# Second normalized rows through DRAM in 32 by 32 blocks, and zeros only behind the ends of the lists

## The chip, the cores and the metric

The kernel runs on one core of a Trainium2 chip. A core has five engines with an instruction stream each: TensorE (PE in the profile) multiplies matrices into PSUM, VectorE (DVE) and ScalarE (ACT) work element by element, GpSimd (POOL) does the same more slowly and issues indirect DMAs, and SyncE (SP) only issues DMAs. Sixteen DMA engines serve all queues. The metric is the device time of one execution in microseconds; lower is better.

## The reference

Four batches of 512 tokens with 512 features, in float32:

```python
x = x + tanh(g_xattn) * attention(layernorm(x), ctx)      # 16 heads of 32, 64 keys, causal mask
xf = layernorm(x)                                         # the "second" normalization
scores = softmax(xf @ gate_w.T); weights, idx = top_k(scores, 2)      # 8 experts
y = sum over the two chosen experts e of weight * (silu(xf @ w1[e].T) * (xf @ w3[e].T)) @ w2[e].T
z = (silu(xf @ ws1.T) * (xf @ ws3.T)) @ ws2.T             # the shared expert, for every token
x = x + tanh(g_ffn) * (y + z)
```

A layernorm subtracts the row's mean and divides by the root of its variance plus 1e-5; it has no learned scale. A product contracts over the features, so TensorE needs the rows turned: features on the partitions, tokens along the free dimension.

## The kernel before

**Attention and routing.** `attention()` makes four passes, b = 0 to 3. Pass b scores the queries of batch b in two halves of two token tiles (`score_products`, `largest`, `exponentials`, `softmax`), turns the probabilities (`transpose_p`) and forms their products with the values (`attend`). Between these it projects the queries of batch b+1 (`project_q`), which keeps TensorE supplied. From pass 1 on it also finishes batch b−1, called `last`: `project_out` adds the attention onto x; `moments` and `deviation` give mean and rstd; `second_rows_of` normalizes its four tiles on VectorE; `turn` transposes them on TensorE, 16 products with the identity, and ScalarE copies them to `x2t[last]`; `gate` multiplies the turned rows with the router's weights, `gate_sum` adds four partial products, and `choose` picks two experts a token in some 26 small VectorE instructions, with `attend` of the pass written between them. In the next pass `route` turns the choice into places (one product counts the tokens ahead within a tile, another the tiles ahead), and GpSimd scatters every row, with its weight and address behind it, to two places of the DRAM table `xg_d`: each expert has a region of 2048 rows there. `softmax` uses GpSimd for its last multiply, so it shares that queue with the scatters. `last_routing()` does the same for batch 3, where `fill(n)` puts n products of the shared expert in between.

**The order inside a row.** `normalize(..., turned=True)` stores a row's 32-blocks with two indices swapped. A later fetch of 128 listed rows in four DMAs (`fetch`), followed by one VectorE instruction that transposes 32 by 32 blocks (`turn` at line 882), then gives the experts turned rows. In this kernel TensorE turns the swapped rows as they are, and so `second_rows` loads the router's weights and the shared expert's first weights (`sh13`) with the same swap, in 4 and 8 DMAs.

**Zero rows.** An expert's list ends inside a tile of 128 rows, and the rest of the tile must hold zeros. Nine DMAs at line 253 write zeros into all of `xg_d`, 17,280 rows of 2112 bytes, and one at line 257 into `y_d`, which collects the experts' results. Every scatter waits for the zero fill.

**Experts.** `tile_table` counts the tiles of each expert on VectorE. Then come 34 tiles of 128 rows (32 at least): `fetch`, `turn`, two up products in 8 instructions of TensorE (`hidden`), the gated product, `turn_g`, `down`, and two indirect adding DMAs by GpSimd. At the end the shared expert's down products and y are added and stored.

**What sets the order.** In attention, routing and experts the streams of TensorE, VectorE, ScalarE and GpSimd follow the program as it is written (`manual_schedule`). SP's order up to the experts is set by a scheduler at build time; each queue executes in order, and an instruction that waits holds up all behind it. `sh13` lies in the memory of `wq_sb` and so waits for the last query product. The experts' weights wait for memory of the attention to come free.

Of the kernel before, what the change touches and what calls it, by code (L numbers as in the profile page):

```python
# [13 lines left out]
F32 = mybir.dt.float32  # L14
I32 = mybir.dt.int32
# [4 lines left out]
P = 128  # L20
# [10 lines left out]
TOPK = 2  # L31
CAP = B * S

MAXT = (TOPK * B * S + NE * (P - 1)) // P
MINT = TOPK * B * S // P
ROWS = NE * CAP + (MAXT - TOPK * B * S // P) * P

# [10 lines left out]
def gated_cross_attention_moe(  # L48
# [48 lines left out]
    y_rows = y_d.rearrange("(r h) d -> r (h d)", h=2)  # L97
    xg_w = dram_disjoint_views(xg_d, TOPK * NT)
    y_w = dram_disjoint_views(y_d, 2)
# [48 lines left out]
    rank = counting("rank", [1, NE], [[-1, NE]], base=NE)  # L148
    region = counting("region", [1, NE], [[CAP, NE]])
    tile_start = counting("tile_start", [1, CAP // P], [[P, CAP // P]])  # L150
# [27 lines left out]
    def normalize(xn, b, t, mv, rstd, turned=False):  # L178
# [7 lines left out]
        )  # L186

    def second_rows(w, c):


        return w[:, c, :].rearrange("(a i) n -> i a n", a=DC)

# [20 lines left out]
    with ExitStack() as attn:  # L213
# [27 lines left out]
        for g in range(HC):  # L241
            for j in range(2):
                nc.sync.dma_start(
                    out=wo_sb[ts(g, HD), j::2, :], in_=wo[ts(2 * (g % 2) + j, HD), g // 2 :: 2, :]
                )
        for c in range(DC):
            nc.sync.dma_start(out=gate_sb[ts(c, HD), :, :NE], in_=second_rows(gate_w, c))

        nc.gpsimd.memset(zeros, 0.0)
        nc.gpsimd.tensor_copy(zeros[:, 0, D : D + 2].bitcast(I32), token[:, NT, :])  # L250
        for lo in range(0, ROWS, CAP):
            n = min(CAP, ROWS - lo) // P
            nc.sync.dma_start(  # L253
                out=xg_d[lo : lo + n * P, :].rearrange("(n p) d -> p n d", p=P),
                in_=zeros.broadcast_to([P, n, ROW]),
            )
        nc.sync.dma_start(
# [149 lines left out]

        def choose(b, pl, between=lambda: None):

# [15 lines left out]
            nc.vector.tensor_tensor(lg, lg, m1.broadcast_to(full), ALU.subtract)  # L425
            between()
            ex = wide("ex")
# [54 lines left out]
        def new_xt():  # L482
            return ab.tile([P, DC, S], F32, tag="xt", name="xt")

        def new_qt():
            return a2.tile([P, DC, S], F32, tag="qt", name="qt")
# [6 lines left out]
        def first_rows(b, rest):  # L493
            rest()
            xn = [a4.tile([P, D], F32, tag="xn", name="xn") for t in range(QT)]
            for t in range(QT):
                normalize(xn[t], b, t, mv1[b], rstd1[b])
            return xn

        def turn(xn, dst):  # L500
            for t in range(QT):
                transpose_rows(xn[t], t, dst)

        def new_stats():
# [21 lines left out]

        def tile_table():

            pn = ps_mm.tile([P, 1, NE], F32, tag="mm", name="pn")
            nc.tensor.matmul(pn[:, 0, :], ones, taken[B], start=True, stop=True)  # L530
            n = small.tile([P, NE, 1], F32, tag="n", name="n")
            nc.vector.tensor_copy(n[:, :, 0], pn[:, 0, :])

            def table(shape, name):
# [30 lines left out]
            nc.vector.tensor_scalar(rows, rows, float(P), None, ALU.mult)  # L565
            nc.vector.scalar_tensor_tensor(rows, expert, float(CAP), rows, ALU.mult, ALU.add)
            row_of = const.tile([P, MAXT], I32, name="row_of")
# [17 lines left out]
        sh13 = const.tile([P, 2, DC, FF], F32, tag="wq_sh", name="sh13")  # L585
        for c in range(DC):
            for w in range(2):
                nc.sync.dma_start(
                    out=sh13[ts(c, HD), w], in_=second_rows(w13[0, :, w], c)
                )  # L590

# [13 lines left out]

        def shared_pair(b, f, between=lambda: None):


            first = shared_half(b, f, 0)
            made = between()  # L610
            second = shared_half(b, f, 1)
            g = gs[b][:, f, :]
            nc.scalar.activation(g, first, AF.Silu)
            return lambda: nc.vector.tensor_tensor(g, g, second, ALU.mult), made

# [15 lines left out]
        def attention():  # L631
            xn = [a4.tile([P, D], F32, tag="xn", name="xn") for t in range(QT)]
            nc.gpsimd.tensor_copy(ctx_sb[:, :, 1, :], ctx_sb[:, :, 0, :])
# [46 lines left out]
            for b in range(B):  # L680
# [41 lines left out]
                if b and more:  # L722
                    project_q(xt, qt_next, range(1))
                elif b:
                    gated, _ = shared_pair(*next(parts))
                    table_of(AF.Exp)
# [7 lines left out]
                if b:  # L734
                    if more:
                        project_q(xt, qt_next, range(1, 2))
                    else:
                        gated()
                    xn2 = new_rows(last)
                    second_rows_of(xn2, last, mv, rstd)  # L740
                softmax(p2)
                if more:
                    softmax(p3)
                if b:
                    transpose_p(p0, prt, 0)
                    transpose_p(p1, prt, 1)
                    turn(xn2, x2t[last])
                if more:
                    project_q(xt, qt_next, range(2, 3))
                    if b + 2 < B:  # L750
                        if b:
                            first_rest = first_moments(b + 2)
                            table_of(AF.Exp)
                        xn = first_rows(b + 2, first_rest)
                    project_q(xt, qt_next, range(3, DC))
                    if b:
                        scored = gate(last)
                else:
                    p3 = exponentials(*p3)
                    softmax(p3)  # L760
                    gated, scored = shared_pair(*next(parts), lambda: gate(last))
                    gated()
                    scores = gate_sum(scored)
                transpose_p(p2, prt, 2)
                if not b:
                    project_values(2)
                elif more:
                    scores = gate_sum(scored)
                transpose_p(p3, prt, 3)
                if not b:  # L770
                    project_values(3)
                attended = []

                def attend_now():
                    attended.append(attend(b, prt))

                if b:
                    chosen = (xn2, *choose(last, scores, attend_now))
                else:
                    attend_now()  # L780
                (at,) = attended
                qt = qt_next
# [7 lines left out]
        def last_routing(at, chosen, parts):  # L790
# [13 lines left out]
            xn2 = addressed([rows_sb[:, ts(t, ROW)] for t in range(QT)], b)  # L804
            mv, rstd = new_stats()
            for t in range(QT):
                project_out(b, at, t)
                if not t:
                    scatter_all(*route(b - 1, *chosen))
                moments(b, mv, t)  # L810
            deviation(mv, rstd)()
            second_rows_of(xn2, b, mv, rstd)
            fill(5)
            turn(xn2, x2t[b])
            fill(1)
            scored = gate(b)
            fill(1)
            chosen = choose(b, gate_sum(scored))
            fill(6)
            scatter_all(*route(b, xn2, *chosen))  # L820
            table = tile_table()
            for _ in filling:
# [280 lines left out]
```

## Time and profile before

| | |
|---|---|
| three runs | 467.15, 469.99, 470.5 us; median 469.99 |
| profiled execution | 469.66 us, span 467.9 us |
| passes 0 to 3 end, at the start of the next scores or out projection | 56.3, 99.2, 147.3, 189.4 us |
| last out projection of batch 3 ends | 203.9 us |
| first expert product | 246.0 us |
| shared down products at the end begin | 430.9 us |
| one expert tile on TensorE | 3.44 + 1.72 + 0.22 us |

The profile is one execution. Its span is the time from the first to the last instruction. Busy shares are means over stages with different limits, so the prediction reads the chain, the timelines and the waits of the stage in question. An operation's line is its line in the kernel before. Float32 products appear as two instructions each in the timelines (x16 for 8 products of 128 by 512), transposes as one.

### The profile page before, as it was taken

The page shows a single profiled execution, that of the slowest core. Times are in us where ns is not written, and L with a number is a line of the kernel's source. Part 1 is how long each engine was busy: PE and PEld are TensorE (multiplying, and loading weights), DVE is VectorE, ACT ScalarE, POOL GpSimd, SP SyncE. Part 2 cuts the span into 40 slices and gives each one's busy share as a digit, 9 for nine tenths or more (in the row PEclk, how much of TensorE's full clock was granted, in tenths as well). Part 3 has the DMA queues.
Part 4 walks back from the last instruction along what each step waited for, and adds up shares of the span by engine and source line. Part 5 has one row for each costly group of instructions (what it writes and reads, how often), then busy time and mean ns, then how long its engine had stood idle before and what let it go on. Part 6 is the DMA issues. An engine that isn't in the chain of part 4 may idle for free.

```text
span 467.9 us, 6177 instructions
## 1 busy us (share of the span) xinstructions
PE 452.7 (97%) x1718; PEld 232.7 (50%) x1718; DVE 253.1 (54%) x604; ACT 131.1 (28%) x245; POOL 178.9 (38%) x188
## 2 busy tenths in 40 slices
PE   6999999999989999999999999999999999999994
PEld 5875555564646465454444444444444444444332
DVE  5659698779905975656421344333343333342485
ACT  3357642762533255413011111111111111111000
POOL 3003321303280374251600555565556565555400
PEclk9999999999997999999999999999999999999998
DMA  8989999999992040799835575666665666544498
GB/s 264 317 305 385 387 385 387 386 387 385 400 340 55 1 164 23 272 406 418 352 75 130 106 122 91 98 101 107 95 101 91 97 105 105 79 50 51 55 376 335
DMA packets 70783, 98.10 MB, mean 210 GB/s; under 512 B 11728, under 2 KB 40144, under 8 KB 69584
## 3 DMA queue, kind: packets, MB, share of 16 engines
q1 hardware_dynamic: 58096, 80.01, 50.9%
q0 software_dynamic: 12352, 17.57, 20.8%
q8 instruction: 17, 0.28, 0.3%
q14 instruction: 30, 0.25, 0.2%
q10 hardware_dynamic: 288, 0.00, 0.0%
HBM read 34.84 MB, written 62.71 MB: 208 GB/s over the span
## 4 chain that ended last, share of the span: by engine, by line
PE 65%; SPq 17%; DMA 7%; issue 4%; DVE 3%; POOL 2%; ACT 0%; DVEq 0%; POOLq 0%
PE ph L897 25%; SPq L253 16%; PE py L924 12%; PE ph L622 6%; PE pd L370 6%; PE ph L596 4%; DMA xg_d<-gs_sb 4%; PE pz L958 3%; DMA wo_sb<-in_wo_dram 2%; POOL xg_d L474 2%; PE pg L916 2%; PE early L596 1%; DVE yk L1028 1%; PE po L359 1%; DVE yk L1047 1%
## 5 line engine op out<-in xcount | busy, mean ns | idle before, releaser
L931 POOL DMA_INDIRECT y_d<-y,meta x68 | 105.6, 1553 | 103.2 <-DVE y L928 60.8
L897 PE MATMUL ph<-w_all,xgt 128*128 x272 | 122.5, 593 | 0.1
L897 PEld LDWEIGHTS ph<-w_all,xgt 128*128 128x128 f32 x272 | 49.1, 190 | 49.6 <-issue 49.5
L338 POOL TENSOR_TENSOR pr<-pr,rs 128x1024 f32<-128x1024 f32 x16 | 30.3, 1903 | 110.5 <-DVE rs L337 94.7
L924 PE MATMUL py<-w_all,gt 128*128 x136 | 63.9, 592 | 0.0
L908 DVE SCALAR_TENSOR_TENSOR g<-sl,w,ph 128x256 f32<-128x256 f32 x34 | 16.3, 481 | 87.4 <-ACT sl L906 87.4
L292 PE MATMUL pq<-xt,wq_sb 128*128 128x512 f32 (+1 forms) x160 | 56.9, 511 | 2.5 <-ACT xt L198 1.6
L370 PE MATMUL pd<-wo_sb,at 128*128 128x512 f32 x128 | 56.1, 595 | 0.0
L906 ACT ACTIVATE sl<-ph 128x256 f32<-128x256 f32 x34 | 13.1, 384 | 109.0 <-PE ph L897 109.0
L292 PEld LDWEIGHTS pq<-xt,wq_sb 128*128 128x128 f32 x160 | 29.7, 190 | 26.4 <-issue 20.1
L924 PEld LDWEIGHTS py<-w_all,gt 128*128 128x128 f32 x136 | 25.8, 190 | 32.5 <-issue 32.5
L928 DVE COPY y<-py 128x512 f32<-128x512 f32 x34 | 23.5, 692 | 27.8 <-PE py L924 27.8
L370 PEld LDWEIGHTS pd<-wo_sb,at 128*128 128x128 f32 x128 | 23.9, 190 | 29.1 <-issue 27.7
L958 PE MATMUL pz<-sh,gs_sb 128*128 128x512 f32 (+1 forms) x68 | 28.1, 570 | 1.4 <-DVE y L928 0.9
L622 PE MATMUL ph<-x2t,sh 128*128 128x512 f32 x64 | 28.6, 596 | 0.0
L918 ACT COPY gt<-pg 128x256 f32<-128x256 f32 x34 | 12.7, 373 | 53.1 <-PE pg L916 53.1
L155 DVE BATCH_NORM_STATS2 st<-x 128x6 f32<-128x512 f32 x32 | 21.8, 680 | 5.6 <-DMA x<-in_x_dram 5.1
L885 DVE STREAM_TRANSPOSE xgt<-xg 128x512 f32<-128x512 f32 x34 | 23.9, 702 | 1.0 <-DMA xg<-xg_d 1.0
L474 POOL DMA_INDIRECT xg_d<-xn,pos x16 | 15.9, 992 | 15.8 <-issue 14.1
L958 PEld LDWEIGHTS pz<-sh,gs_sb 128*128 128x128 f32 x68 | 12.7, 190 | 16.6 <-issue 15.1
L330 ACT ACTIVATE pr<-pr 128x1024 f32<-128x1024 f32 x16 | 16.9, 1058 | 14.2 <-DVE pr L329 11.5
L335 DVE TENSOR_REDUCE sm<-pr 128x16 f32<-128x1024 f32 x16 | 19.1, 1194 | 1.2 <-ACT pr L330 1.2
(167 smaller groups left out, 498.7 us busy)
## 6 DMA issues: line engine op xcount, KB each, us to landing
xg_d<-gs_sb SPq DMA_DIRECT2D x8, 4224.0 KB, 31.4
xg<-xg_d SPq DMA_DIRECT2D x144, 64.0 KB, 2.4
w_all<-in_w_dram SPq DMA_DIRECT2D x8, 1024.0 KB, 15.8
y_d<-gs_sb SPq DMA_DIRECT2D x1, 4352.0 KB, 31.6
w_all<-in_w_dram SPq DMA_DIRECT2D x8, 512.0 KB, 15.9
yk<-y_d SPq DMA_DIRECT2D x8, 512.0 KB, 6.5
out_dram<-yk SPq DMA_DIRECT2D x15, 256.0 KB, 5.1
x<-in_x_dram SPq DMA_DIRECT2D x3, 1024.0 KB, 11.3
```

What stands on the lines that cost most here:

```text
L253: nc.sync.dma_start(out=xg_d[lo : lo + n * P, :].rearrange("(n p) d -> p n d", p=P), in_=zeros.broadcast_to([P, n, ROW]),)
L292: nc.tensor.matmul(pq, wq_sb[:, k, ts(c, P)], xt[:, k, tokens], start=(k == 0), stop=(k == DC - 1),)
L338: nc.gpsimd.tensor_tensor(pr, pr, rs.broadcast_to([P, NH, SK]), ALU.mult)
L370: nc.tensor.matmul(pd, at[:, c, ts(t, P)], wo_sb[:, c, :], start=(c == 0), stop=(c == DC - 1),)
L474: nc.gpsimd.indirect_dma_start(out=xg_w[TOPK * (b * QT + t) + k], out_offset=IndirectOffsetOnAxis(ap=pos[b][:, t, k : k + 1], axis=0), in_ ...
L622: nc.tensor.matmul(ph[:, w, :], sh13[:, w, k, ts(f, P)], x2t[b][:, k, :], start=(k == 0), stop=(k == DC - 1),)
L885: nc.vector.transpose(xgt.rearrange("p c t k -> p t c k"), xg.rearrange("p t (c i) -> p t c i", c=DC))
L897: nc.tensor.matmul(ph, xgt[:, k, :], w13_all[:, ds(e, 1), :, k, :], start=(k == 0), stop=(k == DC - 1),)
L924: nc.tensor.matmul(py, gt[:, f, :], w2_all[:, ds(e, 1), f, :], start=(f == 0), stop=(f == FC - 1))
L928: nc.vector.tensor_copy(y, py)
L931: nc.gpsimd.indirect_dma_start(out=y_w[h], out_offset=IndirectOffsetOnAxis(ap=goes[j][:, h : h + 1].bitcast(I32), axis=0), in_=y[:, ts(h, ...
L958: nc.tensor.matmul(pz, gs[b][:, f, ts(t, P)], sh2[:, f, columns], start=(f == 0), stop=(f == FC - 1),)
```

## The change

The second rows no longer go through TensorE to be turned. After normalization `send` writes a batch's four tiles to a DRAM tensor `xn_d[b]` (256 KB each), `bring` reads them back in blocks of 32 rows by 128 features (512-byte pieces; four DMAs for a batch, or eight in the last routing), and `turn_blocks` transposes 32 by 32 blocks on VectorE, four instructions, into `x2t[b]`. The features now come out in natural order, so `second_rows` goes, and the weights are loaded by one DMA each. The gate product moves behind one or both of the last `transpose_p`, `gate_sum` behind `attend`, and `choose` is no longer split. In the last routing, sends and brings go on ScalarE's queue, the tiles are normalized two by two, and 13 fills stand ahead of the gate product instead of 6. The buffer for the brought rows is that of the first normalized rows in attention, and that of `at` in the last routing.

Each expert's region has 128 rows more. The zero fill shrinks to the 896 rows behind all regions; after the last counts, `fill_ends` reads each list's end into a register on SP and writes 128 zero rows behind it.

In the built program SP's order in attention is: the small fill, the fill of `y_d`; four sends and four brings of batch 0; four sends and two brings of batch 1, the load of `sh13`, two more brings of batch 1; four sends and four brings of batch 2; the experts' weights; eight times a register load and a fill; the fetches.

```diff
+REGION = CAP + P
-ROWS = NE * CAP + (MAXT - TOPK * B * S // P) * P
+ROWS = NE * REGION + (MAXT - TOPK * B * S // P) * P
...
+    xn_d = [dram.tile([S, D], F32, name=f"xn_d{b}") for b in range(B)]
...
-        for c in range(DC):
-            nc.sync.dma_start(out=gate_sb[ts(c, HD), :, :NE], in_=second_rows(gate_w, c))
+        nc.sync.dma_start(out=gate_sb[:, :, :NE], in_=gate_w)
...
-        for lo in range(0, ROWS, CAP):
-            n = min(CAP, ROWS - lo) // P
-            nc.sync.dma_start(
-                out=xg_d[lo : lo + n * P, :].rearrange("(n p) d -> p n d", p=P),
-                in_=zeros.broadcast_to([P, n, ROW]),
-            )
+        n = ROWS // P - NE * REGION // P
+        nc.sync.dma_start(
+            out=xg_d[NE * REGION :, :].rearrange("(n p) d -> p n d", p=P),
+            in_=zeros.broadcast_to([P, n, ROW]),
+        )
...
+        def send(xn, b, tiles=range(QT), queue=nc.sync):
+            for t in tiles:
+                queue.dma_start(out=xn_d[b][ts(t, P), :], in_=xn[t][:, 0:D])
+
+        def bring(xg, b, tiles=range(QT), queue=nc.sync):
+            lo, hi = tiles[0], tiles[-1] + 1
+            for a in range(DC):
+                queue.dma_start(
+                    out=xg[ts(a, HD), lo:hi].rearrange("k t tb n -> k (t tb) n"),
+                    in_=xn_d[b][lo * P : hi * P, ts(a, P)].rearrange("(t k) n -> k t n", k=HD),
+                )
+
+        def turn_blocks(xg, b, tiles=range(QT)):
+            for t in tiles:
+                nc.vector.transpose(
+                    x2t[b][:, :, ts(t, P)].rearrange("p c (tb k) -> p tb c k", k=HD),
+                    xg[:, t].rearrange("p tb (c i) -> p tb c i", c=DC),
+                )
...
+        def fill_ends(n):
+            end = const.tile([P, NE], I32, name="end")
+            nc.vector.tensor_tensor(end, n[:, :, 0], region[:, 0, :], ALU.add)
+            for e in range(NE):
+                r = nc.sync.value_load(end[0:1, e : e + 1], min_val=0, max_val=ROWS - P)
+                nc.sync.dma_start(
+                    out=xg_w[TOPK * NT + e][ds(r, P), :], in_=zeros[:, 0, :]
+                )
...
         sh13 = const.tile([P, 2, DC, FF], F32, tag="wq_sh", name="sh13")
-        for c in range(DC):
-            for w in range(2):
-                nc.sync.dma_start(
-                    out=sh13[ts(c, HD), w], in_=second_rows(w13[0, :, w], c)
-                )
+        nc.sync.dma_start(out=sh13, in_=w13[0])
...
                     second_rows_of(xn2, last, mv, rstd)
+                    send(xn2, last)
+                    xg = ab.tile([P, QT, QT, P], F32, tag="xn", name="xg")
+                    bring(xg, last)
...
-                    turn(xn2, x2t[last])
                 if more:
                     project_q(xt, qt_next, range(2, 3))
+                    if b and b + 2 < B:
+                        first_rest = first_moments(b + 2)
+                        table_of(AF.Exp)
+                    if b:
+                        turn_blocks(xg, last)
...
                     project_q(xt, qt_next, range(3, DC))
-                    if b:
-                        scored = gate(last)
...
-                    gated, scored = shared_pair(*next(parts), lambda: gate(last))
+                    gated = shared_pair(*next(parts))
                     gated()
-                    scores = gate_sum(scored)
+                    turn_blocks(xg, last)
                 transpose_p(p2, prt, 2)
...
                 elif more:
-                    scores = gate_sum(scored)
+                    scored = gate(last)
                 transpose_p(p3, prt, 3)
                 if not b:
                     project_values(3)
+                elif not more:
+                    scored = gate(last)
+                at = attend(b, prt)
                 if b:
-                    chosen = (xn2, *choose(last, scores, attend_now))
+                    chosen = (xn2, *choose(last, gate_sum(scored)))
...
                 moments(b, mv, t)
-            deviation(mv, rstd)()
-            second_rows_of(xn2, b, mv, rstd)
+                if t % 2:
+                    done = range(t - 1, t + 1)
+                    deviation(mv, rstd, done)()
+                    for i in done:
+                        normalize(xn2[i][:, 0:D], b, i, mv, rstd, turned=True)
+                    send(xn2, b, done, nc.scalar)
+            for done in (range(0, 2), range(2, QT)):
+                bring(xg, b, done, nc.scalar)
+            turn_blocks(xg, b, range(0, 2))
+            fill(8)
+            turn_blocks(xg, b, range(2, QT))
             fill(5)
-            turn(xn2, x2t[b])
-            fill(1)
             scored = gate(b)
             fill(1)
             chosen = choose(b, gate_sum(scored))
             fill(6)
-            scatter_all(*route(b, xn2, *chosen))
-            table = tile_table()
+            places, scatter = route(b, xn2, *chosen)
+            n = counted()
+            places()
+            fill_ends(n)
+            for t in range(QT):
+                scatter(t)
+            table = tile_table(n)
```

## The prediction

> **What bounds the kernel now.** First the page, engines and slices: TensorE is busy nearly all the time, at full clock but for one dip.
>
> ```profile
> PE 452.7 (97%) x1718; PEld 232.7 (50%) x1718; DVE 253.1 (54%) x604; ACT 131.1 (28%) x245; POOL 178.9 (38%) x188
> PEclk9999999999997999999999999999999999999998
> DMA  8989999999992040799835575666665666544498
> ```
>
> So a step costs what it takes from TensorE's stream, or what it makes that stream wait. The DMA engines are full for 125 us with the zero fill, but that matters only where TensorE waits. The chain that ended last (start, us, what) and TensorE's timeline (start, us, operation) show where: pass 2, near 137 us.
>
> ```profile
> 98.22 17.87 DMA xg_d<-gs_sb
> 116.09 8.82 issue
> ```
>
> ```profile
> 136.82 1.06 PE L382 MATMUL pg<-x2t,gate_sb 128*32 128x512 f32 x8
> 139.72 1.09 PE L345 MATMUL pp<-ident,pr 128*128 128x128 f32 x8 [1.84 <-POOL pr L338]
> 143.66 3.67 PE L359 MATMUL po<-prt,vals 64*32 64x512 f32 x32
> ```
>
> GpSimd's eight scatters of batch 0 stand in front of its softmax multiply, and wait for the end of the zero fill; TensorE then idles 1.84 us. The windows (PE busy, PEld, DVE, ACT, POOL, clock, DMA share, GB/s) show a second price: about 6.5 us at half clock.
>
> ```profile
> 142.00:144.00 2.00, 2.00 (x16) 1.56 (x23) 1.73 (x10) 0.82 (x2) 0.00 (x0) 0.50 0.70 127
> 146.00:148.00 2.00, 2.00 (x22) 0.74 (x8) 0.00 (x0) 1.42 (x4) 0.00 (x0) 0.51 0.00 0
> 148.00:150.00 2.00, 2.00 (x34) 1.88 (x31) 1.17 (x8) 0.62 (x3) 0.00 (x0) 1.00 0.00 0
> ```
>
> Against the undisturbed pass 1, po is 3.67 instead of 1.95 us, and the score and sum products 0.3 us each longer: 2.35 us.
>
> **What is removed.** (1) 64 transposes of second rows: 16 take 1.75 us of the chain in each of four places, 7.0 us. The ScalarE copies behind them (2.1 us a pass) were hidden. (2) The 34.6 MB of zeros: the scatters no longer wait, so 1.84 us goes. Next late there would be TensorE itself. The half clock goes too only if nothing else stalls this pass. (3) Fewer issues for gate_sb and sh13: nothing, SP waits there.
>
> **The round trip.** The timelines of VectorE and TensorE give normalization and gate product of pass 1:
>
> ```profile
> 81.53 1.91 DVE L184 TENSOR_SCALAR xn<-x,mv,rstd 128x512 f32<-128x512 f32 x4
> 93.30 1.07 PE L382 MATMUL pg<-rows_sb,gate_sb 128*32 128x512 f32 x8
> ```
>
> The answers on the tiles give times from issue to landing: the scatters into xg_d (270 KB, rows of 2112 B) at 163 to 176 us, the same at 195 to 207 us, and the experts' fetches of 64 KB; the page gives VectorE's block transpose.
>
> ```profile
> DMA to landing us min/median/max: 2.7/2.8/2.8
> DMA to landing us min/median/max: 7.7/10.3/13.1
> DMA to landing us min/median/max: 1.8/2.0/3.6
> L885 DVE STREAM_TRANSPOSE xgt<-xg 128x512 f32<-128x512 f32 x34 | 23.9, 702 | 1.0 <-DMA xg<-xg_d 1.0
> ```
>
> Let N be the end of the fourth normalization. A send is near a quiet scatter in size: last issue N+0.5, landed N+3.3. Then four bring issues at about 0.4 us; 2048 packets of 512 B over 16 engines. The queue's share between 280 and 400 us (22.1% of 16 engines, 15,864 packets) makes 27 ns a packet, so 3.4 us of data; with the 1.8 us of a fetch, N+8.9. Four VectorE turns are 2.9 us: rows turned at N+11.8.
>
> The Trainium skill, "DMA: Bandwidth & Descriptors", section "Anatomy of one DMA", gives a fixed 2.0 us plus bytes at 436 GB/s: my estimate by it is 2.6 + 4.4 = 7.0 us for the trip instead of 8.9, and it warns that the receipt from HBM is the slow part. The rows are nearer; 7.0 is the lower end.
>
> **Pass 1.** N = 83.4, turned at 95.2. TensorE reaches the gate at 93.3 − 1.75 (no transposes) + 0.95 (a p transpose moved ahead) = 92.5: stall 2.7 (lower end 0.8). Moreover the sums now come after attend, and route after the 2.0 us of score products. Before, the choice needed 3.9 us from the sums (96.2) to the last count (100.1), under attend:
>
> ```profile
> 96.22 0.19 DVE L421 COPY lg<-pl 128x32 f32<-128x32 f32 x1 [1.19 <-PE pl L393]
> 99.92 0.17 DVE L436 TENSOR_TENSOR taken<-earlier,both 128x8 f32<-128x8 f32 x1
> 101.21 0.41 PE L455 MATMUL pr<-both,before 128*128 128x32 f32 x2
> ```
>
> Now 3.9 − 2.0 = 1.9 us of wait at route; pd and the following passes queue behind it. VectorE's score work starts some 2 us later against TensorE; the row of before had 0.5 us to spare at the fourth pd, so up to 1.5 us more is in the range.
>
> **Pass 2.** SP's built order decides here: four sends, two brings, the load of sh13, then the other two brings. The load waits for the last query product, the last reader of wq_sb:
>
> ```profile
> SPq L588 <- PE pq L292: 23.7, 1, 23.7
> ```
>
> So the last brings are issued about 1.15 us after that product, behind 1 MB in the same queue (2.6 us at 400 GB/s): 1.5 to first data, 2.6, 1.7 for half the rows, 0.4 to land make 6.2, and the turns 2.9, 9.1 us; TensorE has one p transpose, 0.93. Stall 8.2 (4.9 if sh13's data is not ahead of them). Again 1.9 at route.
>
> **Pass 3.** N = 175.7, turned at 187.5. TensorE would be at the gate at 179.9 − 1.75 + 3.5 (second shared half) + 1.75 (p transposes) and 0.5 for the softmax of p3: 183.9. Stall 3.6, plus that 0.5 (lower end together 2.2). At route 3.6 us of pd cover the choice's 3.9: 0.3; the 0.34 us wait of before at this place is dropped. Sum 4.1.
>
> **Last routing.** N is some 4.7 us after the last pd. Sends and brings go on ScalarE's queue, but the DMA engines are full: 398 to 426 GB/s between 195 and 215 us, of the experts' w13 and batch 2's scatters. By bytes (11 MB at 0.4 MB/us from 14.5 us before the last pd) they stay full until about 8 us after N. So a send costs 7.7, not 2.8: N+8.3, four brings issued 2.0, landing 1.8, two turns 1.45: pd+18.3 against 13 fills × 0.86 = pd+11.2. Stall 7.1 (2.2 with 2.8; 12.5 with 13.1). The shared silu queued behind the brings on ScalarE costs nothing: two PSUM pairs last to the sixteenth fill.
>
> **Clock.** The Trainium skill, "TensorE: Matmul & The Clock Gate", section "What's actually happening", says that the clock halves after an idle window of about 3.4 us. The dip above followed 1.84 us, so the measurement decides: I take 2.35 us behind each of the four stalls. By the rule pass 1 would pay nothing. Pass 2 paid already.
>
> **List ends.** Eight loads of `end` and eight DMAs of 270 KB on SP, before the first fetch. The gap between two fetches (236.9 to 237.8) prices a load at 0.85 and an issue at 0.35: 9.6 us, from 2.6 after route to 12.2. The last scatter issue ended at 231.7, 12.7 after route (218.9): hidden. But seven more fills stand ahead of route, so 6.0 us less TensorE work lies behind it. The first xgt was ready at 239.0 and read at 246.0: 7.0 − 6.0 leaves 1.0. I take 0 here, up to 3 in the range. w2's loads now wait for the last turns, because their memory is freed then; they have 20 us until the first down product.
>
> **Sum.** Removed 7.0 + 1.84 = 8.8. Added: pass 1 2.7 + 1.9 + 2.35 = 6.95; pass 2 8.2 + 1.9 = 10.1; pass 3 4.1 + 2.35 = 6.45; last 7.1 + 2.35 = 9.45; together 32.95. Net +24.1 on the profiled execution's 469.66 us (span 467.9), which is 0.3 below the median 469.99: 494.
>
> **Rivals.** *Short trips.* The trip is 7.0 or less and sends in the last routing land as in quiet: stalls 0.8 + 4.9 + 2.2 + 2.2, routes 3.8, one clock dip of 2.35 more: 16.3 − 8.8 = +7.5, 477. For it: quiet landings of 2.8. Against: sh13's place on SP is fixed, and the DMA row at 195 to 215 us. Chance 0.17. *Removal wins.* All four trips are covered by the moved TensorE work; only the two route waits stay: 3.8 − 8.8 − 2.35 (dip gone) = −7.4, 462.5. Its place is the gate product; it decides where the stalls there stay under 7 us in sum, which needs sh13's wait to end some 5 us earlier than the last query product. Chance 0.07. *Late experts.* The fills' data, w2 and scatters collide and the first fetch comes 6 to 10 us later, on top: 503. For it: the 1.0 us left. Chance 0.06. The main case has 0.70.
>
> The range takes in the ends of the costs above, 476 to 508. Within 1% is what a measurement of this kernel can't tell from no change. Faster by over 1% 0.06, within 0.05, slower 0.89.
>
> **What would show it.** TensorE idle before the gate product in all passes, released by a VectorE transpose, longest in pass 2 and in the last routing; sh13's issue between brings at the end of the query products; idle before route of about 2 us in passes 1 and 2; half clock in slices behind; no wait of the scatters at 116 us; expert stage unchanged at 5.37 us a tile. Wrong if the gate finds its rows turned, or if bring's 512 B packets are much slower than 27 ns.

## The result and the profile after

The kernel became slower: 507.87 us median (504.67 to 510.0, four runs) against 468.57 us (466.57 to 470.5, four runs) of the kernel before on the same chip. The ratio is 1.0818, with a 95% interval of 1.0772 to 1.0864. The direction and the place were as forecast; the size was 39.3 us where 24.1 were forecast, and 507.87 lies at the very top of the range; two of the four runs (508.12 and 510.0) lie above it.

The profiled execution took 507.62 us (span 505.5, before 467.9), so 37.6 us of span have to be found. These lines of the page of the kernel after are its span, the engines' busy times and the slices of 12.6 us each.

```profile
span 505.5 us, 6140 instructions
PE 458.8 (91%) x1654; PEld 231.8 (46%) x1654; DVE 264.4 (52%) x627; ACT 125.1 (25%) x231; POOL 178.7 (35%) x188
PEclk9999999879987999799589999999999999999998
DMA  8992002400660037299668367756656656644498
```

TensorE has 64 instructions fewer, the transposes, and is still busy 6 us longer. The row of clocks shows why: it had a single 7 before and now has dips in four places, and in a dip the same product takes nearly twice as long. The full DMA share behind the first slices is gone (98.10 MB moved before, 74.06 MB after); it had cost little, as e1 below shows.

The groups by line put the idle time of TensorE where the prediction had it, in front of the gate product:

```profile
L378 PE MATMUL pg<-x2t,gate_sb 128*32 128x512 f32 x24 | 5.8, 1057 | 26.0 <-DVE x2t L520 26.0
L520 DVE STREAM_TRANSPOSE x2t<-xg 128x512 f32<-128x512 f32 x12 | 7.6, 684 | 30.6 <-DMA xg<-xn_d 30.6
```

After the bar come total busy time and the mean of one (in ns), then the idle time ahead and what ended it. Passes 2 and 3 and the last routing have 26.0 us before the gate, released by VectorE's block transpose, which in turn waited 30.6 us for the brought rows. Pass 1 stands under another buffer's name (`rows_sb`); its wait is marked `issue`, but VectorE's last turn there ends at 97.10, 0.1 us ahead of the gate. TensorE's timeline of the kernel after (start, duration, and in brackets the idle time ahead) has the four gates, `route` in pass 3 and the first expert product. (In all timelines pg is the gate, pp the transposes of p, po `attend`, pl `gate_sum`, psc the scores, pr `route`, pt the transposes of first rows, pd the out projection, ph an up product of the experts or the shared expert.)

```profile
97.20 1.93 PE L378 MATMUL pg<-rows_sb,gate_sb 128*32 128x512 f32 x8 [3.43 <-issue]
...
154.55 1.93 PE L378 MATMUL pg<-x2t,gate_sb 128*32 128x512 f32 x8 [9.26 <-DVE x2t L520]
...
164.31 0.38 PE L450 MATMUL pr<-both,before 128*128 128x32 f32 x2 [1.18 <-DVE earlier L429]
...
204.85 1.94 PE L378 MATMUL pg<-x2t,gate_sb 128*32 128x512 f32 x8 [5.30 <-DVE x2t L520]
...
247.88 1.93 PE L378 MATMUL pg<-x2t,gate_sb 128*32 128x512 f32 x8 [11.48 <-DVE x2t L520]
...
283.30 3.67 PE L936 MATMUL ph<-w_all,xgt 128*128 x8 [1.72 <-issue]
```

All four gates wait, 29.5 us in all, and each then takes 1.93 us instead of 1.06: they run at half clock (0.50 in the windows around them). The same starts, read in both timelines, say where the 37.6 us arose:

| from | before | after | grown by |
|---|---|---|---|
| first scores of pass 0 | 27.1 | 28.4 | 1.3 |
| scores of pass 1 | 56.3 | 57.5 | 0.0 |
| scores of pass 2 | 99.2 | 104.8 | 4.4 |
| scores of pass 3 | 147.3 | 161.1 | 8.2 |
| first out projection of the last routing | 189.4 | 210.6 | 7.3 |
| first expert product | 246.0 | 283.3 | 16.1 |

What is left behind the first expert product is within 0.4 us. The 1.3 us at the start belong to neither half of the change: in this execution the first products (pk) took 3.75 us instead of 1.97. The profile of e1 below, which keeps the transposes, has the same (3.75, first scores at 28.47), and that of e6, which has the trips, has not (1.97, first scores at 26.89).

### The profile page after: what moved, and what is told of

It is laid out like the page before. It is cut to its first block, busy times and chain, and to the rows that moved or that the text cites. A ratio compares the mean times of both kernels' runs of the same rounds, so it can differ in the third digit from the quotient of the medians.

```text
span 505.5 us, 6140 instructions
## 1 busy us (share of the span) xinstructions
PE 458.8 (91%) x1654; PEld 231.8 (46%) x1654; DVE 264.4 (52%) x627; ACT 125.1 (25%) x231; POOL 178.7 (35%) x188
## 2 busy tenths in 40 slices
DMA packets 65185, 74.06 MB, mean 146 GB/s; under 512 B 12144, under 2 KB 47728, under 8 KB 63856
## 4 chain that ended last, share of the span: by engine, by line
PE 72%; DVE 12%; DMA 7%; issue 3%; ACT 2%; POOL 2%; SPq 1%; ACTq 0%; DVEq 0%; POOLq 0%
PE ph L936 23%; PE py L963 12%; PE pq L288 8%; PE pd L366 8%; PE ph L651 4%; DMA xg<-xn_d 3%; PE pz L997 3%; PE ph L626 3%; DMA xn_d<-rows_sb 2%; PE po L355 2%; DVE yk L1067 2%; POOL xg_d L469 2%; PE psc L302 2%; PE pg L378 2%; PE pg L955 1%
## 5 line engine op out<-in xcount | busy, mean ns | idle before, releaser
L651 PE MATMUL ph<-x2t,sh 128*128 128x512 f32 x64 | 31.1, 641 | 0.0
L378 PE MATMUL pg<-x2t,gate_sb 128*32 128x512 f32 x24 | 5.8, 1057 | 26.0 <-DVE x2t L520 26.0
L957 ACT COPY gt<-pg 128x256 f32<-128x256 f32 x34 | 12.6, 372 | 52.8 <-PE pg L955 52.8
L520 DVE STREAM_TRANSPOSE x2t<-xg 128x512 f32<-128x512 f32 x12 | 7.6, 684 | 30.6 <-DMA xg<-xn_d 30.6
L326 ACT ACTIVATE pr<-pr 128x1024 f32<-128x1024 f32 x16 | 16.9, 1058 | 17.5 <-DVE pr L325 13.1
L997 PEld LDWEIGHTS pz<-sh,gs_sb 128*128 128x128 f32 x68 | 12.7, 190 | 17.0 <-issue 15.5
```

Source lines behind the costliest of these rows:

```text
L326: nc.scalar.activation(pr, pr, AF.Exp, scale=1.0 / math.sqrt(HD))
L651: nc.tensor.matmul(ph[:, w, :], sh13[:, w, k, ts(f, P)], x2t[b][:, k, :], start=(k == 0), stop=(k == DC - 1),)
L997: nc.tensor.matmul(pz, gs[b][:, f, ts(t, P)], sh2[:, f, columns], start=(f == 0), stop=(f == FC - 1),)
```

## The experiments

All ratios are against the kernel before on the same chip, with a 95% interval. Two variants take the change apart, four test single waits, one joins three of these, two look for what can be kept; e10 repeats e1. The kernel after was not run again beside the variants, so a difference from its 507.87 us is good to about 1.5 us: against the medians of their own kernels before, the kernel after costs 39.3 us, e3 34.7, e6 29.5, e7 36.1 and e9 22.1.

**The zeros alone (e1).** The kernel before, with the larger regions, the small fill and `fill_ends`; the rows are still turned by TensorE.

```diff
+REGION = CAP + P
-        for lo in range(0, ROWS, CAP):
...
+        n = ROWS // P - NE * REGION // P
...
-            scatter_all(*route(b, xn2, *chosen))
-            table = tile_table()
+            places, scatter = route(b, xn2, *chosen)
+            n = counted()
+            places()
+            fill_ends(n)
+            for t in range(QT):
+                scatter(t)
+            table = tile_table(n)
```

> The kernel before with only the second half of the change: zeros behind the list ends instead of the full zero fill, rows still turned on TensorE. Theory (the scatters' wait for the zero fill cost 1.84 us and a clock dip of 2.35, and the eight end fills hide behind the scatters): 4 us faster than before, 464 to 466, no idle of TensorE before transpose_p of p2 in pass 2, and no wait before the first expert product. Rival (the end fills hold up the first fetch, as the 1.7 us wait of the changed kernel suggests): 468 to 471.

Measured 464.87 us against 467.54, ratio 0.9947 (0.9922 to 0.9972). A repeat, e10, beside e8 below:

> The kernel before with the end fills alone once more, beside the run with early rows on the same chip. Both theories: 464 to 466.

It gave 465.09 us over ten runs, ratio 0.9945 (0.9923 to 0.9967). The page of e1 has no dip of the clock any more, and TensorE's timeline has the transposes of p behind the gate without a wait, where the kernel before idled 1.84 us for GpSimd.

```profile
PEclk9999999999999999999999999999999999999998
```

```profile
139.19 1.09 PE L345 MATMUL pp<-ident,pr 128*128 128x128 f32 x8
```

So the half of the change that concerns zeros gains about 2.5 us, less than the 4.2 us that the theory took from the profile, though from the first scores to the first expert product the two profiles differ by 4.8 (218.9 and 214.1). The reason lies in the kernel before. Its profiled execution had a mean granted clock of 0.99. Of the 48 executions of it that ran beside the variants, nine had a clock of 0.992 or less and took 470.0 us in the mean; the other 39 took 467.0, and the 17 of e1 and e10 took 465.1. In most executions, then, e1 saves about the 1.84 us of the wait, and the half clock behind it seems to belong to a minority of executions, of which the profile caught one. Only that one was traced, so this rests on the clocks and times alone.

The other half, the trip through DRAM, costs more than the whole.

**The trip alone (e2).** The kernel after, with the full zero fill and without `fill_ends`.

```diff
-REGION = CAP + P
+REGION = CAP
...
+        for lo in range(0, ROWS, CAP):
...
-            fill_ends(n)
```

> The changed kernel with the full zero fill put back and the end fills taken out. Theory (a queue's data move in order, so sends of pass 1 on SP's queue stand behind the 34 MB of zeros until about 116 us): the gate product of pass 1 comes some 25 us later, 530. Rival (the trip only shares bandwidth with the zeros): stall of pass 1 up by 5 to 10, 512 to 518. If the zero half of the change is what costs, below 500.

Measured 552.56 us (two runs), ratio 1.1814 (1.1741 to 1.1887): the direction of the theory, and about 22 us more than it expected. SyncE's timeline of e2 (start, duration of the issuing, instruction) and TensorE's show it:

```profile
23.08 84.33 SPq L250 DMA_DIRECT2D xg_d<-gs_sb  x9
...
112.39 15.07 SPq L506 DMA_DIRECT2D xn_d<-xn  x4
```

```profile
145.16 1.93 PE L379 MATMUL pg<-rows_sb,gate_sb 128*32 128x512 f32 x8 [51.62 <-issue]
```

The nine fill instructions occupy SP's instruction stream for 84 us, and the sends, which the kernel after issues from 83.37, are issued only at 112.39; the brings follow at 135.05. On SP's queue the trip needs the small fill in front of it, so the two halves of the change are not independent. A trip beside the full fill on another queue was not tried.

**`sh13` behind the brings (e3).** In the kernel after, the load is issued in pass 2 behind its last query products:

```diff
-        nc.sync.dma_start(out=sh13, in_=w13[0])
...
+                    if b + 2 == B:
+                        nc.sync.dma_start(out=sh13, in_=w13[0])
```

> The changed kernel with the load of sh13 issued behind all four brings of pass 2 instead of between them. Theory (the second pair of brings waited for the last query product and for 1 MB ahead of it): stall before the gate of pass 2 falls from 9.3 to about 4 us, as in pass 1, total 5 us less, 503. Rival (the trip itself is that slow in pass 2): 508.

Measured 502.2 us, ratio 1.0722 (1.0683 to 1.0761), about 5 us less than the kernel after (5.7 by the medians, 4.6 against its own kernel before). The chain of work that ended last (start, us, what) runs through this place in the kernel after:

```profile
137.45 6.98 PE pq L288 x16
144.44 0.35 SPq L620
...
144.84 0.43 SPq L512
...
145.31 6.57 DMA xg<-xn_d
...
151.91 2.50 DVE x2t L520 x4
...
154.55 1.93 PE pg L378 x8
```

The last query products release `sh13` (line 620), the load releases the last brings (line 512), and these land behind it. TensorE's timeline of e3 has the shorter stall:

```profile
147.74 1.94 PE L378 MATMUL pg<-x2t,gate_sb 128*32 128x512 f32 x8 [4.47 <-DVE x2t L520]
```

Of pass 2's 9.26 us, 4.8 are the place of one instruction in SP's queue. The rest is the trip itself, as in the other passes, and the theory's 4 us was right.

**The experts' weights behind the brings (e4).** The w13 loads, which keep the DMA engines full in the last routing, are issued on ScalarE's queue behind the last bring.

```diff
                 bring(xg, b, done, nc.scalar)
+            w13_all = load_w13()
...
-                nc.sync.dma_start(out=w13_all[:, e], in_=w13[1 + e])
...
+                    nc.scalar.dma_start(out=w13_all[:, e], in_=w13[1 + e])
```

> The changed kernel with the experts' w13 loads (8 MB) issued on ScalarE's queue behind the last brings, not on SP at the end of attention. Theory (sends and brings of the last routing shared the DMA engines with w13): stall before the last gate falls from 11.5 to about 4 us, 500. Rival 1 (the trip is that long without them): 508. Rival 2 (the weights now come late and the first expert product waits): the stall falls, the time does not, 508 to 515.

Measured 508.87 us over four runs, 506.5 without the longest of them, ratio 1.085 (1.078 to 1.0921): indistinguishable from the kernel after. This is the second rival, the wait moved. The gate's wait falls from 11.48 to 6.95 us and the experts' rises from 1.72 to 10.61. (The profiled execution is that longest one, 513.15 us, so its waits may be a little long.) The chain of e4, and SyncE's timeline:

```profile
228.51 2.57 DMA xn_d<-rows_sb
...
233.62 0.46 ACTq L873
...
239.33 0.61 ACT gs_sb L633
...
240.56 1.31 DVE x2t L520 x2
...
274.70 3.79 DMA xg_d<-gs_sb
...
283.64 6.70 PE ph L940 x8
```

```profile
242.06 21.93 SPq L882 DMA_DIRECT2D w_all<-in_w_dram  x8
265.34 9.69 SPq L562 DMA_DIRECT2D xg_d<-gs_sb  x8
```

Without the loads the last rows are sent in 2.57 us; in the kernel after this piece of the chain is 11.70. More than half of what is left of the stall is of e4's own making: eight weight issues stand on ScalarE's queue in front of a silu of the fills, VectorE's product with that silu stands in front of the last two turns, and so the turns start at 240.56. The rows would have been turned at 237.5 (an estimate: the last bring issued at 232.8, a median landing of 3.4 us, two turns of 1.3), not at 241.9. And then w2's eight issues occupy SP for 21.93 us, behind w13's data, with the fills of the list ends and the fetches queued behind them: the first fetch is issued at 278.81, in the kernel after at 278.42. A version with both of these orders mended was not tried.

**The router's sums ahead of `attend` (e5).** To take away the wait before `route`:

```diff
+                if b:
+                    sums = gate_sum(scored)
                 at = attend(b, prt)
                 if b:
-                    chosen = (xn2, *choose(last, gate_sum(scored)))
+                    chosen = (xn2, *choose(last, sums))
```

> The changed kernel with the partial sums of the router ahead of attend again, so that the choice runs under attend. Theory (route waits 1.4 us in passes 1 and 2 because the choice starts late, and a second clock dip follows in pass 1): both waits gone, 3 to 4 us less, 504. Rival (VectorE is then the later engine and the wait only moves): 507 to 508.

Measured 510.0 us, ratio 1.0878 (1.0817 to 1.0938): no gain. The wait is gone, but the same products are longer. TensorE's timeline of pass 1, first the kernel after (its gate is shown above), then e5:

```profile
100.96 2.96 PE L355 MATMUL po<-prt,vals 64*32 64x512 f32 x32
103.85 1.06 PE L389 MATMUL pl<-part,parts 128*128 128x8 f32 x8
...
108.07 0.38 PE L450 MATMUL pr<-both,before 128*128 128x32 f32 x2 [1.18 <-DVE earlier L429]
```

```profile
95.76 1.07 PE L378 MATMUL pg<-rows_sb,gate_sb 128*32 128x512 f32 x8 [3.40 <-issue]
...
98.41 1.71 PE L389 MATMUL pl<-part,parts 128*128 128x8 f32 x8
100.05 3.67 PE L355 MATMUL po<-prt,vals 64*32 64x512 f32 x32
...
105.66 0.41 PE L450 MATMUL pr<-both,before 128*128 128x32 f32 x2
```

In e5 the gate itself is at full clock and the half clock falls on pl (1.71 instead of 1.06) and po (3.67 instead of 2.96) behind it. From the start of the gate to route it is 10.87 us in the kernel after and 9.90 in e5: 1.0 us came free. In the next pass the same stretch is longer, 9.76 us and 10.70, with po at 3.52 instead of 1.95, and the last gate waits 12.90 us instead of 11.48.

**The clock kept up (e6).** Dummy products fill the waits ahead of the four gates. They write the PSUM tile that the gate overwrites, and nobody reads them; no data comes earlier by it.

```diff
+            for _ in range((3, 10, 5, 12)[b]):
+                nc.tensor.matmul(pg, ident, xs[b ^ 3][:, 0, :], start=True, stop=True)
```

> The changed kernel with products that nobody reads put into the four stalls ahead of the gate product (3, 10, 5 and 12 of 128 by 512, 0.86 us each, sized to end before the rows are there). Theory (TensorE's clock is halved after each stall because TensorE was idle, 12 us in all): full clock behind the gate products, stalls unchanged in place, 10 us less, 498. Rival (the half clock comes from something else, or the time behind the stalls is waiting and not clock): 507 to 510.

Measured 497.61 us, ratio 1.061 (1.0545 to 1.0676): about 10 us less than the kernel after (10.3 by the medians, 9.8 against its own kernel before), with more work. The mean granted clock rises from 0.953 to 0.995. TensorE's timeline of e6:

```profile
141.10 8.75 PE L378 MATMUL pg<-x,ident 128*128 128x512 f32 x20
...
151.24 1.06 PE L380 MATMUL pg<-x2t,gate_sb 128*32 128x512 f32 x8 [1.38 <-DVE x2t L522]
```

The gate is back at 1.06 us. So the half clock behind these waits costs about 10 us of the 39, and most of the rest is the waits themselves.

**e3, e4 and e5 together (e7).**

> The changed kernel with three repairs together: sh13 behind the brings, w13 behind the last brings, sums ahead of attend. If the parts add: 508 minus 5, 8 and 3, 492. If the waits only move to the next late thing: 497 to 503. Below 469 only if the trip is hidden everywhere, which neither theory expects.

Measured 504.22 us, ratio 1.0764 (1.0693 to 1.0835): less gain than even the reading with moved waits expected, and no more than e3 alone. The last gate still waits 7.42 us and the first expert product 8.02, then at half clock. The order on SP is that of e4: w2's issues from 233.91 for 21.65 us, the fills of the list ends only behind them, and the first fetch at 270.67.

**The last routing back on TensorE (e9).** Passes 1 to 3 keep the trip; batch 3 is normalized once more without the swap and turned by 16 transposes, with fills 5 and 1 around them as before.

```diff
-                    send(xn2, b, done, nc.scalar)
-            for done in (range(0, 2), range(2, QT)):
-                bring(xg, b, done, nc.scalar)
-            turn_blocks(xg, b, range(0, 2))
-            fill(8)
-            turn_blocks(xg, b, range(2, QT))
...
+                normalize(plain[:, t, :], b, t, mv, rstd)
+            second_rows_of(xn2, b, mv, rstd)
             fill(5)
+            turn([plain[:, t, :] for t in range(QT)], x2t[b])
+            fill(1)
             scored = gate(b)
```

> The changed kernel with only the last routing taken back: batch 3 is turned on TensorE, with 6 fills ahead of its gate product. Theory (the last routing is the largest single loss: 11.5 us stall, 4.3 us at half clock, 1.7 us wait before the first expert product, against 1.75 us of transposes): 16 us less, 492. Rival (a stall there only used time that the experts' loads needed anyway): 500 or more.

Measured 489.15 us, ratio 1.0449 (1.039 to 1.0508). TensorE's timeline of e9 has no wait at the gate, none at the first expert product:

```profile
230.56 1.06 PE L378 MATMUL pg<-x2t,gate_sb 128*32 128x512 f32 x8
...
265.90 3.67 PE L931 MATMUL ph<-w_all,xgt 128*128 x8
```

So 507.87 − 489.15 = 18.7 us of the 39.3 belong to the trip of the last routing (17.2 by the kernels before of the two chips), the wait of the first expert product with it. The 22.1 us that e9 is still slower than the kernel before belong to the three other trips.

**Rows sent early (e8).** What remains of the idea when each wait that was found is mended: e9's last routing, e3's `sh13`, the sums ahead of `attend` in passes 1 and 2, and above all normalization, sends and brings directly behind rstd (made by `rest()`), ahead of VectorE's softmax work.

```diff
                     rest()
+                    xn2 = new_rows(last)
+                    second_rows_of(xn2, last, mv, rstd)
+                    send(xn2, last)
...
+                    bring(xg, last)
                 p2 = exponentials(*p2)
...
-                    second_rows_of(xn2, last, mv, rstd)
-                    send(xn2, last)
...
-                    bring(xg, last)
```

> The changed kernel with the trip kept in passes 1 to 3 and made to fit: the second rows are normalized and sent straight after rstd, some 3.6 us (passes 1 and 2) and 5 us (pass 3) earlier on VectorE; sh13 behind the brings; the sums ahead of attend in passes 1 and 2; and batch 3 in the last routing turned on TensorE as before, from a second, unswapped normalization. Theory (the loss is rows that come late, not the trip as such, and the gain is 1.75 us of TensorE in each pass without a stall): the gate products of passes 1 to 3 wait 0 to 1 us each, clock full, 465 minus 5.25 plus 1, 461. Rival (the trip always costs more than the transposes, since contention with scatters makes it longer): 466 to 472.

Measured 466.79 us over 22 runs, ratio 0.9989 (0.997 to 1.0008): level with the kernel before, and slower than e1, whose repeat e10 ran on the same chip (465.09). The gates hardly wait any more (0, 0.43, 2.03 us) and the clock is 0.996, so the 5.25 us of transposes in three passes are gone. But VectorE's softmax is now later, and with it the work behind: in pass 1 ScalarE's second exponential waits for VectorE until 83.61, and its copy of the queries follows at 84.58. TensorE's timeline of e8 has new waits at the transposes of p, for that copy (0.92 us in pass 1, 1.23 in pass 2) and for VectorE in pass 3 (0.60), beside the 2.03 us left at pass 3's gate.

```profile
85.19 0.66 PE L341 MATMUL pp<-ident,pr 128*128 128x128 f32 x4 [0.92 <-ACT qt L292]
...
180.45 1.06 PE L378 MATMUL pg<-x2t,gate_sb 128*32 128x512 f32 x8 [2.03 <-DVE x2t L520]
...
241.24 3.60 PE L936 MATMUL ph<-w_all,xgt 128*128 x8
```

The first expert product starts at 241.24; in e1 it starts at 242.57, but e1's profile is late by 1.4 us from its first scores on (28.47 and 27.06). From first scores to first expert product both take the same, 214.2 and 214.1 us: the five waits come to 5.2 us, as much as the transposes that are gone. Whether a finer order of VectorE's and ScalarE's work would keep the rest was not tried.

## Why the prediction was right in its direction and too small

The prediction held in its mechanism: TensorE waits before the gate in all passes, longest in pass 2 and the last routing; `sh13` stands between brings; route waits in passes 2 and 3 for the batch before; half clock follows; the zero fill's wait at 116 us is gone. It was wrong in the sizes of its sum, most of them too small, and that 507.87 still lies inside the range, by 0.13 us, is luck. In us, by the timelines:

| term | forecast | measured |
|---|---|---|
| transposes removed | −7.0 | −7.0 |
| scatter wait and its half clock | −1.84, −2.35 | −1.84, −3.2 |
| gate of pass 1, 2, 3, last | 2.7, 8.2, 3.6, 7.1 | 3.43, 9.26, 5.30, 11.48 |
| softmax of p3 | 0.5 | 0.79 |
| route, three places | 1.9, 1.9, 0.3 | 1.39, 1.39, 0 |
| wait ahead of po in pass 3 | −0.34 | −0.34 |
| half clock, all waits | 9.4 | 10 (e6) to 12.3 (products) |
| first expert product | 0 | 1.72 |
| start | 0 | 1.3 |

The measured column, with 12.3, adds up to 36.0 of the 37.6 us of span; what is missing are shifts of less than 0.5 us each. (The forecast entered three dips of 2.35 net, since one was there before; here it is five dips less that one. 12.3 is the lengthening of the products behind the waits, read one by one; e6's gain of about 10 is net of a wait of the first expert product of 3.90 us where the kernel after has 1.72.)

**Step "The round trip": the brings were mis-sized.** The sends were right: N was 84.7, the first bring was issued at 87.58, 2.9 later, with 3.3 forecast. The turns took 2.49 us, with 2.9 forecast. But the rows landed 7.0 us behind the first bring, not 5.6. VectorE's timeline of the kernel after, pass 1 (four normalizations, then four turns):

```profile
82.80 1.91 DVE L187 TENSOR_SCALAR xn<-x,mv,rstd 128x512 f32<-128x512 f32 x4
...
94.61 2.49 DVE L520 STREAM_TRANSPOSE rows_sb<-xg 128x512 f32<-128x512 f32 x4 [3.62 <-DMA xg<-xn_d]
```

With the 1.8 us of a fetch taken off, 5.2 us remain for 128 pieces of 512 B on each of 16 engines: an estimate of 41 ns a piece instead of the 27 that the expert stage had given. That 27 was a mean over 15,864 packets, of which, by an estimate from 89 fetches of 64 KB, about 11,400 were pieces of 512 B and the rest smaller. The prediction had named this as a way to be wrong. The brings are late in all four places, by 0.9 to 1.4 us; in pass 3 the send was late as well, landing 4.2 us behind N (191.02 to 195.20) instead of 3.3. Shorter turns gave 0.4 us back, and the gates of passes 1 to 3 came out 0.7 to 1.7 us late each.

From N to the landed rows it was 9.9 us, where the prediction had 8.9 and, as the lower end, 7.0 by the Trainium skill. The section behind the 7.0 ("DMA: Bandwidth & Descriptors", "Anatomy of one DMA — SWDGE (gpsimd) path") fits DMAs issued by GpSimd, and these were issued by SP; the measurement decides.

**Step "Last routing": the largest miss, 4.4 us.** The turned rows were put 18.3 us behind the end of the last out projection (pd); they came at pd+22.6. The chain and the windows of the kernel after (in the windows PE, PEld, DVE, ACT and POOL busy, clock, DMA share, GB/s):

```profile
229.85 11.70 DMA xn_d<-rows_sb
...
241.90 0.31 ACTq L512
...
243.26 3.05 DMA xg<-xn_d
...
246.43 1.32 DVE x2t L520 x2
```

```profile
230.00:235.00 5.00, 5.00 (x13) 2.14 (x12) 0.00 (x0) 0.00 (x0) 0.00 (x0) 1.00 1.03 424
235.00:240.00 5.00, 1.40 (x4) 0.33 (x2) 0.00 (x0) 0.00 (x0) 0.00 (x0) 0.96 1.01 408
240.00:245.00 5.00, 0.00 (x0) 0.00 (x0) 1.26 (x2) 1.17 (x1) 0.00 (x0) 0.50 0.83 186
```

With N at 229.8, the send was to have landed at N+8.3 and landed at N+11.8: 3.5 of the 4.4 us. The brings took 4.7 us instead of 3.8, the other 0.9. The row that the step rested on had 7.7, 10.3 and 13.1 us as least, median and most, and the step took the least, with a guess by bytes of how long the DMA engines would be full; they were full until 240, not 238. The mechanism is shown: the send takes 11.70 us here, 10.90 in e6, and 2.57 in e4, which has no loads beside it. In addition the half clock lasted from 240 to about 257 us (clock 0.50 in the window from 250 to 255 us too), since gate, sums and fills all follow a long wait; by products it cost 4.3 us, not 2.35.

**Step "Clock": right to decide by the trace, and too small.** The 2.35 us left out one product of the dip that it was read from. Behind the wait of before, the second half of the transposes of p is at half clock too; TensorE's timeline of the kernel before has it in pass 1 and in pass 2:

```profile
96.03 1.07 PE L345 MATMUL pp<-ident,pr 128*128 128x128 f32 x8
...
141.79 1.95 PE L345 MATMUL pp<-ident,pr 128*128 128x128 f32 x8
```

So that dip cost 3.2 us. Of the 12.3 us of the kernel after, 10.7 are behind the four gates (2.9, 1.5, 2.0 and 4.3), and 1.6 are a fifth dip that the forecast did not have, behind route's wait in pass 2, where pd took 14.85 us instead of 14.00:

```profile
108.91 2.72 PE L195 MATMUL pt<-ident,xn 128*128 128x128 f32 x16
```

Behind the same wait in pass 3 pd took 13.98, so there was no such dip; in e4 it was the other way round (14.00 in pass 2, 15.68 in pass 3). The Trainium skill, "TensorE: Matmul & The Clock Gate", "What's actually happening", asks for an idle window of about 3.4 us; pass 1's wait of 3.43 is at that bound and did halve the clock, in the kernel after as in e5 with 3.40, but so did 1.84 in the profile of before and 1.39 ahead of this pt. The measurement decides: behind short waits the half clock came in some executions and not in others, behind gate waits of 3.07 us and more always, and it added about a third to them.

**Step "Pass 2": right.** The stall was 9.26 against 8.2, and e3 splits it as the prediction did: forecast 8.2 to 4.9 without `sh13`, measured 9.26 to 4.47. (The 4.9 does not follow from the step's own terms: without the 2.6 us of `sh13` they give 5.6.)

**Route: 2.8 instead of 4.1.** The forecast let route wait for the last count, 3.9 us behind the sums. In the trace its first product is released earlier, by the copy `earlier` (line 429), 2.9 us behind them (104.95 to 107.84 in VectorE's timeline).

**Step "List ends": 1.72 instead of 0,** inside the 3 us that the range allowed. The forecast had the last fill issued 12.2 us behind route, in front of the last scatter (12.7). The scatter held to that; the eight loads and fills took 11.97 us, not 9.6, and ended at 275.46, 15.2 us behind route, and the first fetch followed at 278.42. e1 and e9 have the same fills and no such wait; both have seven more fills of the shared expert behind route, which are the prediction's 6.0 us.

**The rivals.** *Short trips* (477) and *Removal wins* (462.5) fell with the landings. *Late experts* (503) was right in its place and too large there. That the measured time is above its 503 has other reasons and is no support for it.

## What to carry to other kernels

A trip that takes work from a busy engine must be costed to the moment when that engine can use the rows, with each of its transfers under the traffic of its own moment and each of its instructions at its own place in the queue; 7.0 us of transposes were exchanged for 29.5 us of waits. Waits of an engine that was hardly ever idle cost more than their length when the clock falls behind them, here about a third more, so products that fill a wait that can't be removed are worth a trial. Read a cost of that kind from more than one execution: the dip of the profiled kernel before seems not to have been in most of its executions. And take a change with two halves apart: the smaller half of this one, zeros only behind the ends, is a little faster than the kernel before (464.87 us, ratio 0.9947, and 0.9945 in the repeat), while the large half hid it.

## What the runs showed of the hardware

While the DMA engines were full, issuing a DMA held up its queue's instruction stream, and not only the data path (DMA share 1.01 to 1.06 from 20 to 107 us in e2, 1.01 to 1.02 from 240 to 265 in e4): SP spent 84.33 us issuing nine fills in e2, with sends ready behind them 29 us late, and 21.93 us issuing w2's eight loads in e4 (3.73 in the kernel after). The price of one small transfer ranged with the traffic beside it: the last two tiles of 256 KB were sent in 2.57 us and in 11.70. Pieces of 512 B from DRAM cost about 41 ns each per DMA engine when a batch was brought in quiet (an estimate from 7.0 us of landing), against a mean of 27 ns over the packets of the expert stage, smaller ones among them. Waits of TensorE ahead of the gate, from 3.07 us in e9 to 51.62 in e2, were all followed by products at half clock. After the start of the gate the clock was low for 3 us in pass 2, 4 in pass 3, 6 in pass 1, and 9 behind the wait of 11.48 us with its small dependent products (until about 257 us). Of the shorter waits, 1.84 us in before, 1.39 ahead of pt in the kernel after and 2.10 ahead of the experts in e5 were followed by it; 2.03 at a gate of e8 was not, and neither were 3.90 ahead of the experts in e6. About 10 us of an execution came and went with the clock alone (507.87 to 497.61).
